# Attention and involution on one core: how the sums of exponentials get across the partitions in the first three images

## The chip, the cores and the metric

The kernel runs on one core of a Trainium2 chip. The metric is the device time in microseconds, the median of several runs of the same program; lower is better. The engines are TensorE (PE, with its weight loads shown apart as PEld), VectorE (DVE), ScalarE (ACT), GpSimd (POOL) and the DMA queues, most of them issued by SyncE (SP).

## What is computed

Input `x` has 4 images of 512 channels and 64 x 64 pixels in float32. Two layers follow each other. The reference, cut:

```python
# layer 0: attention over the 4096 pixels of an image, 128 inner channels
q, k, v = (einsum('oc,bcn->bon', w, xf) + b[:, None] for w, b in ...)
attn = softmax(einsum('bci,bcj->bij', q, k), axis=-1)
out = einsum('bcj,bij->bci', v, attn)
x = einsum('oc,bcn->bon', wo, out) + bo[:, None] + x
# layer 1: involution, 7 x 7 taps, groups of 16 channels
o1 = relu(affine(conv1x1(x, W1), s1, b1))
w  = conv1x1(relu(affine(conv1x1(o1, Wr), sr, br)), Ws) + bs
y  = sum over the 49 taps of w[group, tap, pixel] * o1[channel, pixel shifted by the tap]
out = affine(conv1x1(y, W3), s3, b3) + x
```

The softmax is computed without subtracting a maximum. (A check at the end of the kernel branches to a second, general path where the sums leave a safe interval; with these inputs that path is not taken.)

## The kernel before

**Attention.** The images are worked on one after the other. For each, `keys_values` makes the keys (`pk`) and values (`pv`) of all 4096 pixels. Then `attention` goes through eight chunks of 512 queries, numbered 0 to 7. A chunk has 32 steps. Step j makes one block of scores for 128 keys (`pss`, a matmul with 512 columns), ScalarE takes the exponential (`pt`, L797), and TensorE adds values times exponentials to `po`. The scores run two steps ahead. VectorE adds each `pt` to `pacc` (L826, L828, and for the last step to `sums`, L831), so that at the end of a chunk `sums` holds, for each of its 128 partitions, partial sums of the exponentials of 512 queries.

**The end of a chunk.** `finish_block` is a generator, started at the end of the chunk and advanced between the steps of the next one, one `yield` at a time; `chores()` does it once a step. It copies `po` to `on` (ScalarE, L651). It adds up `sums` over the partitions: L654, a VectorE reduction with a built-in transposition in blocks of 32 x 32, leaves in `blocks` 16 columns, and in each quarter of 32 partitions the sums over that quarter alone. In the kernel before, a matmul with `quads` (a matrix of ones wherever two partitions have the same place in their quarters) then adds the four quarters, and every partition gets the total (`pl`). After that come the reciprocal (L663, into `rls`), a transposition that spreads it over the columns (`spread` in PSUM, L666), and the product `on` times `spread` (L670). Next are the output projection (`pwo`) with the residual added on VectorE (L679), `p1` with its ReLU on ScalarE (L699), a transposition of the result into pixels and its way out by DMA (L732), and `pr`, which makes the units of the involution available.

The pauses in it differ between images. In the last image (`late`) they wait until a planned time; in the first three they are a number of `yield`s: three between the reduction and `pl`, five between the product `on` and the residual.

**Involution.** A unit is 4 lines of an image, 16 units an image. `involution` records its taps between the attention's steps: VectorE makes a product (L427, out of PSUM tile `pw` with the weights, of which there is one buffer), GpSimd adds it to `acc` (L447) and at the end folds it (L462). Then VectorE transposes the unit's sums (`turned`, L508), two DMAs finish the transposition, and `py` (TensorE) with its eviction on VectorE (L577) closes a chunk of output.

**What sets the order.** The program is recorded in the order of the generators, and a scheduler then places each engine's instructions by its own estimates; the engines work through their queues in order. How fast the taps are recorded is set by a planner: `pe` is the planned time of TensorE, `free["dve"]` and `free["pool"]` are the planned times when VectorE and GpSimd come free, `takes(engine, us)` adds work to them, and a tap waits while VectorE is planned to be 3.5 us or more behind.

**Buffers.** `pl`, `spread`, `pwo`, `p1`, `pr`, `py` and the queries (`pq`, made in step 23 or so of the chunk before) take turns in two PSUM banks (tag `mm`). `po` and `pacc` have one bank each. Five buffers hold exponentials.

Of the kernel before, what the change touches and what calls it, by code (L numbers as in the profile page):

```python
# [8 lines left out]
F32 = mybir.dt.float32  # L9
AF = mybir.ActivationFunctionType  # L10
ALU = mybir.AluOpType
# [4 lines left out]
P = 128  # L16
CT = C // P
CH = 512
# [62 lines left out]
TB = 32  # L81
# [8 lines left out]
def fast_path(  # L90
# [20 lines left out]
    nc = tc.nc  # L111

    def pool(name, bufs, **kw):
        return ctx.enter_context(tc.tile_pool(name=name, bufs=bufs, **kw))
# [6 lines left out]
    work2 = pool("work2", 2)  # L121
# [5 lines left out]
    ps = pool("ps", 2, space=bass.MemoryType.PSUM)  # L127
# [15 lines left out]
    quads = const.tile([P, P], F32, name="quads")  # L143
# [24 lines left out]
    free = {"dve": 0.0, "pool": 0.0, "dma": 0.0}  # L168
# [8 lines left out]
    def until(us):  # L177
        while pe < us and not tail:
            yield "wait"

    def pe_us(us):
        nonlocal pe
        pe += us
# [27 lines left out]
    def takes(engine, us):  # L211
        free[engine] = max(free[engine], pe) + us
        return free[engine]
# [39 lines left out]
    def mm(o, lhsT, rhs, start=True, stop=True, shared=1):  # L253
        pe_us(rhs.free_size() * PE_COLUMN / shared)
        return nc.tensor.matmul(o, lhsT=lhsT, rhs=rhs, start=start, stop=stop)  # L255
# [380 lines left out]
    def finish_block(b, c, off, n, po, sums):  # L636

        late = b == B - 1
        direct = late and c >= DIRECT
        name = f"{b}_{c}_{off}"  # L640
        xt = xs[b, c][:, :, off : off + n]

        def pause(us, steps):
            if late:
                yield from until(us + HOP_US)
            else:
                for _ in range(steps):
                    yield

        on = work2.tile([P, CH], F32, tag="on", name=f"on_{name}")[:, :n]  # L650
        nc.scalar.copy(on, po)  # L651
        blocks = work2.tile([P, CH // TB], F32, tag="blocks", name=f"blocks_{name}")
        takes("dve", DVE_OP)
        nc.vector.tensor_reduce(  # L654
            blocks, sums.rearrange("p (k q) -> p k q", q=TB), AX.X, ALU.add, apply_transpose=True
        )
        yield from pause(free["dve"], 3)
        pl = ps.tile([P, CH // TB], F32, tag="mm", name=f"pl_{name}")[:, : n // TB]
        for i in range(CH // n):
            mm(pl, quads, blocks[:, i * n // TB : (i + 1) * n // TB], i == 0, i == CH // n - 1)  # L660
        row = (b * N + c * CH + off) // TB
        rl = rls[:, row : row + n // TB]
        nc.vector.reciprocal(rl, pl)  # L663

        spread = ps.tile([P, CH], F32, tag="mm", name=f"spread_{name}")[:, :n]
        nc.vector.transpose(  # L666
            spread.rearrange("p (k q) -> p k q", q=TB),
            rl.unsqueeze(2).broadcast_to([P, n // TB, TB]),
# [59 lines left out]
        else:  # L728

            blocks = o1t.rearrange("p t c -> p (t c)")  # L730
# [48 lines left out]
    def attention(b, kt, vT, q):  # L779
# [22 lines left out]
        for m, (k, j) in enumerate(steps):  # L802
# [22 lines left out]
            if j == 0:  # L825
                nc.vector.tensor_copy(paccs[k], pt)  # L826
            elif j < nj - 1:
                nc.vector.tensor_tensor(paccs[k], paccs[k], pt, ALU.add)  # L828
            else:
                sums = work1.tile([P, CH], F32, tag="sums", name=f"sums_{b}_{k}")  # L830
                nc.vector.tensor_tensor(sums, paccs.pop(k), pt, ALU.add)  # L831
                f = finish_block(b, c, off, n, pos.pop(k), sums)
                next(f)
                finishing.append(f)
# [445 lines left out]
```

## Time and profile before

| | |
|---|---|
| median of 3 runs | 2587.23 us (2586.75 to 2587.34) |
| profiled execution | 2587.14 us, of which span 2585.2 us |
| granted TensorE clock | 0.999 |
| TensorE busy | 2570.4 us, 99% of the span |
| VectorE busy | 1862.6 us, 72% |
| GpSimd busy | 1825.2 us, 71% |
| ScalarE busy | 838.2 us, 32% |
| mean DMA rate | 94 GB/s |

The span runs from the first instruction to the last of the profiled execution; the time around it belongs to the launch. A matmul in float32 is carried out in two passes, and each shows as one weight load and one MATMUL row. The durations of matmuls are modelled, so their starts are what is read here. In the rows, `out<-in` names what is written and what is read; an idle time in brackets is followed by what ended it. "issue" is time in which an engine waited for nothing that the profile shows.

Chunk boundaries can be found by the copies of `po` (L651): in image 0 they begin at 125.87, 193.25, 260.63, 332.49, 405.84, 476.00, 547.86 and 616.30 us.

### The profile page before, as it was taken

The page shows a single profiled execution, that of the slowest core. Times are in us where ns is not written, and L with a number is a line of the kernel's source. Part 1 is how long each engine was busy: PE and PEld are TensorE (multiplying, and loading weights), DVE is VectorE, ACT ScalarE, POOL GpSimd, SP SyncE. Part 2 cuts the span into 40 slices and gives each one's busy share as a digit, 9 for nine tenths or more (in the row PEclk, how much of TensorE's full clock was granted, in tenths as well). Part 3 has the DMA queues.
Part 4 walks back from the last instruction along what each step waited for, and adds up shares of the span by engine and source line. Part 5 has one row for each costly group of instructions (what it writes and reads, how often), then busy time and mean ns, then how long its engine had stood idle before and what let it go on. Part 6 is the DMA issues. An engine that isn't in the chain of part 4 may idle for free.

```text
span 2585.2 us, 24342 instructions
## 1 busy us (share of the span) xinstructions
PE 2570.4 (99%) x7367; PEld 1229.3 (48%) x7367; DVE 1862.6 (72%) x2678; ACT 838.2 (32%) x1386; POOL 1825.2 (71%) x1207
## 2 busy tenths in 40 slices
PE   9999999999999999999999999999999999999998
PEld 7444444445544444444554444444465444444476
DVE  0347778887585777888667667878857678787888
ACT  1333333332233333333223333333322333333331
POOL 0006788877881778888786368888788567887887
PEclk9999999999999999999999999999999999999999
DMA  6033233445615343234661434433364431332343
GB/s 238 1 74 62 58 77 83 98 102 148 151 60 114 64 102 69 68 81 99 166 153 41 108 69 96 102 70 92 79 181 112 110 90 47 90 78 61 78 95 101
DMA packets 209049, 243.36 MB, mean 94 GB/s; under 512 B 109640, under 2 KB 129040, under 8 KB 208784
## 3 DMA queue, kind: packets, MB, share of 16 engines
q1 hardware_dynamic: 208480, 241.39, 38.9%
q8 instruction: 59, 0.97, 0.2%
q14 instruction: 78, 0.64, 0.1%
q10 hardware_dynamic: 432, 0.36, 0.1%
HBM read 192.65 MB, written 49.06 MB: 93 GB/s over the span
## 4 chain that ended last, share of the span: by engine, by line
PE 92%; POOL 4%; DVE 3%; issue 1%; ACT 0%; DVEq 0%; POOLq 0%
PE pss L255 32%; PE po L255 31%; PE pv L255 4%; PE pk L255 4%; PE pq L255 4%; PE p L255 4%; PE pwo L255 4%; PE py L255 4%; POOL acc L447 4%; PE pw L255 2%; DVE prod L427 1%; DVE pacc L828 1%; PE pr L255 1%; PE pa L259 1%; POOL acc L462 0%
## 5 line engine op out<-in xcount | busy, mean ns | idle before, releaser
L447 POOL TENSOR_TENSOR acc<-acc,prod 128x768 f32<-128x768 f32 (+3 forms) x1052 | 1682.8, 1617 | 737.9 <-DVE prod L427 694.6
L255 PE MATMUL pss<-q,k 128*128 128x512 f32 (+1 forms) x2112 | 1055.7, 584 | 0.0
L255 PE MATMUL po<-pt,v 128*128 128x512 f32 (+1 forms) x2112 | 1047.3, 580 | 0.0
L797 ACT ACTIVATE pt<-pss 128x512 f32<-128x512 f32 x1024 | 611.1, 597 | 1242.6 <-PE pss L255 1188.8
L427 DVE TENSOR_TENSOR prod<-ring,pw 128x768 f32<-128x768 f32 (+3 forms) x1086 | 874.7, 840 | 46.0 <-POOL acc L447 44.9
L828 DVE TENSOR_TENSOR pacc<-pacc,pt 128x512 f32<-128x512 f32 x958 | 664.8, 694 | 237.9 <-ACT pt L797 209.9
L255 PEld LDWEIGHTS po<-pt,v 128*128 128x128 f32 x2112 | 398.8, 190 | 480.9 <-issue 460.4
L255 PEld LDWEIGHTS pss<-q,k 128*128 128x128 f32 x2112 | 391.4, 190 | 466.8 <-issue 462.0
L508 DVE STREAM_TRANSPOSE turned<-acc 128x256 f32<-128x256 f32 x48 | 21.4, 445 | 217.9 <-POOL acc L462 217.9
L255 PE MATMUL py<-accT,wt 128*128 128x512 f32 (+1 forms) x256 | 130.1, 590 | 4.5 <-DVE x L577 4.5
L255 PE MATMUL pwo<-on,wt 128*128 128x512 f32 (+1 forms) x264 | 128.6, 580 | 0.1
L462 POOL TENSOR_TENSOR acc<-acc 128x512 f32<-128x512 f32 x122 | 121.4, 995 | 9.6
L255 PEld LDWEIGHTS pv<-wt,x 128*128 128x128 f32 x1024 | 119.6, 192 | 15.3 <-issue 15.1
L577 DVE SCALAR_TENSOR_TENSOR x<-py,vec,x 128x512 f32<-128x512 f32 (+2 forms) x136 | 96.4, 711 | 36.2 <-PE py L255 35.7
L255 PE MATMUL pv<-wt,x 128*128 128x128 f32 x1024 | 120.2, 275 | 0.0
L255 PE MATMUL p<-x,wt 128*128 128x512 f32 (+1 forms) x264 | 119.3, 580 | 0.0
L255 PE MATMUL pk<-x,wt 128*128 128x512 f32 x256 | 117.1, 596 | 0.0
L706 ACT ACTIVATE x<-x,vec 128x512 f32<-128x512 f32 (+1 forms) x132 | 92.9, 706 | 74.2 <-PE p L255 58.1
L255 PE MATMUL pq<-x,wt 128*128 128x512 f32 (+1 forms) x264 | 115.3, 579 | 0.0
L679 DVE SCALAR_TENSOR_TENSOR x<-pwo,bo,x 128x512 f32<-128x512 f32 (+1 forms) x132 | 95.1, 727 | 21.3 <-PE pwo L255 19.9
L427 DVE TENSOR_TENSOR acc<-ring,pw 128x1024 f32<-128x1024 f32 (+1 forms) x85 | 78.7, 945 | 15.6 <-PE pw L255 15.6
L255 PEld LDWEIGHTS pq<-x,wt 128*128 128x128 f32 x264 | 50.1, 190 | 59.7 <-issue 56.4
(74 smaller groups left out, 727.0 us busy)
## 6 DMA issues: line engine op xcount, KB each, us to landing
x<-x_dram SPq DMA_DIRECT2D x55, 1024.0 KB, 5.7
ring<-pix SPq DMA_DIRECT2D x74, 448.0 KB, 7.0
ring<-pix SPq DMA_DIRECT2D x24, 1344.0 KB, 9.7
out_dram<-x SPq DMA_DIRECT2D x31, 1024.0 KB, 4.5
ring<-pix SPq DMA_DIRECT2D x24, 896.0 KB, 10.5
ring<-pix SPq DMA_DIRECT2D x30, 672.0 KB, 10.9
ring<-pix SPq DMA_DIRECT2D x6, 2240.0 KB, 19.5
pix<-o1t SPq DMA_DIRECT2D x192, 32.0 KB, 1.7
```

Of the source, the lines that this page charges most:

```text
L255: return nc.tensor.matmul(o, lhsT=lhsT, rhs=rhs, start=start, stop=stop)
L259: nc.tensor.matmul(o, lhsT=lhsT, rhs=ident, start=start, stop=stop, is_transpose=True)
L427: product = (nc.gpsimd if maker == "pool" else nc.vector).tensor_tensor(made.rearrange("p t d (g c) -> p t d g c", g=G), image.rearrange(" ...
L447: nc.gpsimd.tensor_tensor(acc[:, these, d0 : d0 + n, :], acc[:, these, d0 : d0 + n, :], prod[:, :nt, :n, :], ALU.add,)
L462: nc.gpsimd.tensor_tensor(acc[:, :, :n, :], acc[:, :, :n, :], acc[:, :, n : 2 * n, :], ALU.add)
L508: nc.vector.transpose(blocks.rearrange("p (t k q) -> p t k q", t=NT, q=TB), acc[:, :, 0, :].rearrange("p t (k q) -> p t k q", q=TB),)
L577: nc.vector.scalar_tensor_tensor(xt[:, t, :], py, v1(V_S3 + t), xt[:, t, :], ALU.mult, ALU.add)
L679: nc.vector.scalar_tensor_tensor(xt[:, t, :], pw, bo[:, t : t + 1], xt[:, t, :], ALU.add, ALU.add)
L706: nc.scalar.activation(xt[:, t, :], xt[:, t, :], AF.Identity, bias=v1(V_B3 + t))
L797: nc.scalar.activation(pt, pss, AF.Exp)
L828: nc.vector.tensor_tensor(paccs[k], paccs[k], pt, ALU.add)
```

## The change

In images 0 to 2 the four quarters are no longer added by the matmul. VectorE copies `blocks` into the first columns of the PSUM tile `spread`, adds each quarter's neighbour to it (four adds on 32 partitions of 16 columns), copies the pair sums to PSUM again, adds the other pair's (two adds on 64 partitions), and takes the reciprocal in place in `rls`. The second operand of an add lies in PSUM, so that it can come from other partitions. The three pauses ahead of `pl` are gone in these images, and the whole chain up to the product `on` is recorded in one go at the end of the chunk. The planner is told of 1 us more on VectorE. In the last image nothing changes.

```diff
         blocks = work2.tile([P, CH // TB], F32, tag="blocks", name=f"blocks_{name}")
+        blocks2 = work2.tile([P, CH // TB], F32, tag="blocks2", name=f"pairs_{name}")
         takes("dve", DVE_OP)
         nc.vector.tensor_reduce(
             blocks, sums.rearrange("p (k q) -> p k q", q=TB), AX.X, ALU.add, apply_transpose=True
         )
-        yield from pause(free["dve"], 3)
-        pl = ps.tile([P, CH // TB], F32, tag="mm", name=f"pl_{name}")[:, : n // TB]
-        for i in range(CH // n):
-            mm(pl, quads, blocks[:, i * n // TB : (i + 1) * n // TB], i == 0, i == CH // n - 1)
+        if late:
+            yield from pause(free["dve"], 3)
         row = (b * N + c * CH + off) // TB
         rl = rls[:, row : row + n // TB]
-        nc.vector.reciprocal(rl, pl)
+        if late:
+            pl = ps.tile([P, CH // TB], F32, tag="mm", name=f"pl_{name}")[:, : n // TB]
+            for i in range(CH // n):
+                mm(pl, quads, blocks[:, i * n // TB : (i + 1) * n // TB], i == 0, i == CH // n - 1)
+            nc.vector.reciprocal(rl, pl)
 
         spread = ps.tile([P, CH], F32, tag="mm", name=f"spread_{name}")[:, :n]
+        if not late:
+            cols = n // TB
+            other, pairs = spread[:, :cols], blocks2[:, :cols]
+            nc.vector.tensor_copy(other, blocks)
+            for i in range(P // TB):
+                mine, next_ = (slice(j * TB, (j + 1) * TB) for j in (i, i ^ 1))
+                nc.vector.tensor_tensor(pairs[mine], blocks[mine], other[next_], ALU.add)
+            nc.vector.tensor_copy(other, pairs)
+            for i in range(2):
+                mine, next_ = (slice(j * 2 * TB, (j + 1) * 2 * TB) for j in (i, i ^ 1))
+                nc.vector.tensor_tensor(rl[mine], pairs[mine], other[next_], ALU.add)
+            nc.vector.reciprocal(rl, rl)
+            takes("dve", 1.0)
         nc.vector.transpose(
             spread.rearrange("p (k q) -> p k q", q=TB),
             rl.unsqueeze(2).broadcast_to([P, n // TB, TB]),
```

## Prediction

> **What bounds the kernel now.** I read the page first: busy time, then the chain that ended last.
>
> ```profile
> PE 2570.4 (99%) x7367; PEld 1229.3 (48%) x7367; DVE 1862.6 (72%) x2678; ACT 838.2 (32%) x1386; POOL 1825.2 (71%) x1207
> ...
> PE 92%; POOL 4%; DVE 3%; issue 1%; ACT 0%; DVEq 0%; POOLq 0%
> ```
>
> TensorE carries 92% of the chain, and POOL and DVE carry only the tail. Cut into stages, the profile has TensorE busy for 1827.02 of the 1831.00 us between 129 and 1960 us, which are images 0 to 2 after the first keys. So there a matmul less is time gained, and every wait that is put before a matmul is time lost. The order of the changed kernel's instructions is the same as before from chunk 1 of image 3 on, on TensorE, so the tail stays; all that follows is three times the same image.
>
> Then TensorE's timeline around one `pl`:
>
> ```profile
> 128.33 1.02 PE L255 MATMUL po<-pt,v 128*128 128x512 f32 x2
> 129.19 0.29 PE L255 MATMUL pl<-blocks,quads 128*128 128x16 f32 x2
> 129.33 1.10 PE L255 MATMUL pss<-q,k 128*128 128x512 f32 x2
> 130.27 0.59 PE L255 MATMUL po<-pt,v 128*128 128x512 f32 x1
> ```
>
> A product of 512 columns starts every 0.86 us (128.33 to 129.19; I use 0.859). From one `po` to the next lie 1.94 us here where a pair without `pl` takes 1.72: `pl` costs 0.22 us, more than its 0.14 alone, since its second weight load cannot hide behind so short a product.
>
> Third, what TensorE's waits are. The four idle microseconds of that stage are three of these, one in each image:
>
> ```profile
> 379.24 0.65 PE L255 MATMUL pr<-o,wt 128*64 128x256 f32 x4
> 381.02 1.12 PE L255 MATMUL py<-accT,wt 128*128 128x512 f32 x2 [1.12 <-DVE x L577]
> 382.36 0.93 PE L255 MATMUL pw<-wt,red 33*128 33x392 f32 x4 [0.22 <-DVE prod L427]
> ```
>
> The second `py` of chunk 4 wants the PSUM buffer of the first, whose eviction (L577) is late in VectorE's queue.
>
> Last, VectorE at the end of a chunk, the tightest one:
>
> ```profile
> 406.04 0.68 DVE L831 TENSOR_TENSOR sums<-pacc,pt 128x512 f32<-128x512 f32 x1
> 406.75 0.71 DVE L654 TRANSPOSE_TENSOR_REDUCE blocks<-sums 128x16 f32<-128x512 f32 x1
> 407.39 0.67 DVE L826 COPY pacc<-pt 128x512 f32<-128x512 f32 x1
> ...
> 411.03 0.25 DVE L663 RECIPROCAL rls<-pl 128x16 f32<-128x16 f32 x1
> ...
> 412.00 0.71 DVE L666 STREAM_TRANSPOSE spread<-rls 128x512 f32<-128x512 f32 x1
> ...
> 413.48 0.67 DVE L670 TENSOR_TENSOR on<-on,spread 128x512 f32<-128x512 f32 x1
> ```
>
> `on` is ready at 414.15; the weights of the first `pwo` load at 417.54, 3.4 us later. Over the 24 chunks this margin is 3.4 to 6.8 us, and it is what the change spends.
>
> **Removed: 24 `pl`.** 24 x 0.22 = 5.3 us, all on the path. Nothing hides it.
>
> **Moved: the residual, three steps earlier.** Without the three pauses the first `pwo` stands after step 3 or 4 of the next chunk (4 in chunks 3, 4, 6; 3 in 0, 1, 2; one product earlier than 4 in 5), where it stood after step 6. `p1`, `pr`, the pixel DMAs and the units follow; the DMAs have 11 steps or more to their reader in both orders, so I cost them at nothing. Counted from the copy of `po` (405.84 in the chunk shown), the slot of the first `pwo` was 417.54 - 405.84 = 11.70 us. It becomes 11.70 - 0.22 - 4 x 0.859 = 8.04 for chunks 3, 4, 6, 6.3 for 0 to 2, 7.2 for 5.
>
> **Moved with it: the late eviction of `py`.** In the new order `pr` and the first `py` stand together at step 18, the second `py` at step 20 behind other buffers, and the first eviction has four steps. The wait of 1.12 us and what surrounds it go. Its price is read from the copies of `po`: chunks 2 to 3 and 5 to 6 are 71.86 us apart (332.49 - 260.63, 547.86 - 476.00), chunks 3 to 4 are 73.35 (405.84 - 332.49). 1.49 x 3 = 4.5 us. What may be late next: the queries of step 23 need the buffer of the second `py`, whose eviction stands behind the transposition that waits for POOL's last fold (L508; 204.6 us of waits on VectorE in this stage). In the chunk above that transposition began 19.6 us before the copy, and about 19.4 is needed. The units start about 2 us earlier in the new order, which gives that margin.
>
> **Added: eight small VectorE instructions a chunk,** in one chain from the reduction to `on`. The trace has none of them. The nearest rows: an add of 128x4 took 0.164 us, the reciprocal of 128x16 took 0.25; the adds of 512 columns take 0.694 but start every 0.605, so 0.09 overlap. Lower end 0.09 each (all overlapped), 0.7 us a chunk; upper end 0.28 each (the reciprocal and a dependent start, 0.03), 2.2 us. Less than nothing is excluded: no instruction goes from VectorE. I take 0.19, from the add, the nearest row: 1.5 us. 24 x 1.5 = 36 us more on VectorE, 72% to 73.5%: no bound.
>
> The Trainium skill ("VectorE: DVE Perf Modes", on two Vector instructions with no wait between them) speaks against this: an instruction whose operands start in another group of 32 partitions than those of the one before waits until all earlier ones have finished. By it the six adds would not overlap, nor would the next large instruction, some 0.2 us a chunk more than my value; the sum for the path would change only in chunks without margin. No row here shows such adds.
>
> **Does `on` come in time?** In the new order of chunks 3, 4 and 6, five adds of the next chunk and one tap product stand among the chain. From the start of `sums`: 0.71 + 0.64 + 0.57 for sums, reduction, copy; 5 x 0.605 adds; 0.86 product (407.96 to 408.82); 0.16 reciprocal (to its successor); 0.63 transposition; 0.67 product; 1.5 small ones: 8.8 us (8.0 to 9.5). Chunk 5: 7.7 to a slot of 7.2. Chunk 2: 7.3 to 6.3. Chunks 0, 1 and 7 have no taps in the way and microseconds of margin.
>
> So it hangs on when `sums` starts, relative to the copy of `po`: -3.6 us in chunks where VectorE only waits for exponentials, +0.2 in the chunk shown, the latest of all. VectorE is backlogged from the transposition (386.25) to `sums` (406.04). In the new order its queue there holds 1.5 to 5 us more work, but the unit before began earlier (step 8 for 10 or 11), so the transposition is earlier too. By these I get starts at about -3 (chunk 3), -1.5 (4), -2 (5), -1 (6), and in chunk 2 -3: `on` at 5.8, 7.3, 5.7, 7.8, 4.3 against 8.0, 8.0, 7.2, 8.0, 6.3. It just fits; chunk 6 has 0.2 us. I allow 0.7 us of waits an image, 2 us.
>
> **Sum.** Profiled execution 2587.14 (span 2585.2, 1.9 around it; the median of three is 2587.23, 0.1 more): 2587.2 - 5.3 - 4.5 + 2 = 2579.4. Below all this lies 2577.4 with no wait at all.
>
> **Rivals.** *The matmul alone.* The wait of `py` does not go but moves to the queries, or small waits of 1.5 us an image before `pwo` eat it: 2587.2 - 5.3 = 2581.9, and up to 2592 as these waits grow to 5 us an image. For it: L508's waits of up to 7.3 us. Against: the units' earlier start.
>
> *`on` is late: slower.* One mechanism: the chain ends after the slot of the first `pwo`, and TensorE stands; behind the waiting `pwo` queue the next scores, and ScalarE's exponentials and VectorE's adds wait for those. If `sums` starts at +0.2 in chunks 2 to 6, as in the tightest chunk now, and a small instruction takes 0.28: 0.2 + 9.5 - 8.0 = 1.7 in chunks 3, 4, 6; 0.2 + 8.4 - 7.2 = 1.4 in 5; 0.2 + 8.0 - 6.3 = 1.9 in 2. That is 8.4 an image, 25 us, and 2602 in all. It decides from 3.3 us an image (9.8 / 3) on. For it: 3.4 us of margin in the tightest chunk are less than the 3.66 by which its slot moves. Against: `on` no longer waits for `pl` (VectorE waited 9.8 us for it in this stage) and the earlier units.
>
> *VectorE or POOL becomes the bound:* it would need some 500 us more; no chance worth a number.
>
> **Chances.** A measurement of this kernel can tell some 0.2%, 5.2 us, from no change. The forecast (both gains, under 1.5 us of waits an image) 0.6; the matmul alone or less 0.26, of which 0.02 beyond 0.2%; late `on` beyond its gain 0.14. Faster by over 0.2% (below 2582.1): 0.62; within: 0.24; slower: 0.14. The range goes from 2576.5, just under the case without waits, to 2590, which takes in most of the second case and leaves out the third.
>
> **What would show it.** Right: no `pl` before 1960 us, TensorE's 1.12 us waits for L577 gone, chunks 71.6 us apart, small adds of 0.16 to 0.2 us. Wrong: weight loads of `pwo` that wait for L670's successor, weight loads of `pq` that wait for L577's, each with its lateness; then chunks 2 to 6 are longer than 0 and 1.

## The result, and the profile after

| | before | after |
|---|---|---|
| median | 2587.28 us (6 runs) | 2605.78 us (2604.09 to 2608.14, 6 runs) |
| ratio after to before | | 1.0071, 95% interval 1.0058 to 1.0083 |
| profiled execution | 2587.14 us, span 2585.2 | 2608.14 us, span 2606.3 |
| first and last (24th) copy of `po` of images 0 to 2 | 125.87, 1881.22 us | 126.58, 1900.76 us |

The changed kernel is slower by 0.7%; the forecast was 2579.4 us. The medians are 18.5 us apart. The profiled executions, of which that of the changed kernel is the slowest of its six, are 21.1 us apart in span, of which 18.8 lie between the first and the 24th copy of `po` (1774.18 us for 1755.35). The start is 0.7 us later, image 3 is 0.4 shorter, and 1.9 come behind the last work of any compute engine.

The page, its busy times and its chain that ended last:

```profile
PE 2575.7 (99%) x7319; PEld 1228.4 (47%) x7319; DVE 1898.9 (73%) x2870; ACT 838.1 (32%) x1386; POOL 1823.6 (70%) x1207
...
PE 76%; POOL 9%; DVE 8%; issue 5%; DMA 1%; SPq 0%; ACT 0%; POOLq 0%; DVEq 0%
```

The 48 rows that `pl` took from TensorE are gone (7319 for 7367), VectorE has 192 more, and its busy time rose by 36.3 us. That it is close to the 36 of the prediction is in part luck: the eight new instructions of a chunk make 32.2 us of it, and the tap products, which overlap less than before, another 7.0 (881.7 us for 874.7), while smaller groups fell. But the chain has moved: TensorE carries 76% of it instead of 92%, and VectorE and GpSimd 17% instead of 7%. TensorE now waits for them, and the waits between 129 and 1985 us say where (engine, what it was to do, whom it waited for: us in all, times, longest):

```profile
DVE prod L427 <- POOL acc L447: 72.7, 109, 2.0
...
PEld pwo L255 <- DVE on L686: 30.7, 16, 4.3
...
PE pwo L255 <- DVE on L686: 17.8, 14, 3.5
```

The same two kinds of wait before the change, in the same stretch:

```profile
DVE prod L427 <- POOL acc L447: 32.0, 53, 1.8
...
PE py L255 <- DVE x L577: 3.3, 3, 1.1
```

The wait of `py` for L577 is gone. In its place the first `pwo` of a chunk waits for the product `on` (L686): `on` is late. Above it stands a wait that is more than twice what it was: VectorE's tap products wait for one of the four buffers that GpSimd must empty.

Both are seen in chunk 5, the worst one. VectorE's timeline from its tap products to `on`:

```profile
466.48 4.40 DVE L427 TENSOR_TENSOR prod<-ring,pw 128x1024 f32<-128x1024 f32 x5
470.80 0.69 DVE L844 TENSOR_TENSOR pacc<-pacc,pt 128x512 f32<-128x512 f32 x1
472.67 0.69 DVE L427 TENSOR_TENSOR prod<-ring,pw 128x512 f32<-128x512 f32 x1 [1.18 <-POOL acc L447]
473.27 0.69 DVE L844 TENSOR_TENSOR pacc<-pacc,pt 128x512 f32<-128x512 f32 x1
475.10 0.42 DVE L427 TENSOR_TENSOR prod<-ring,pw 128x256 f32<-128x256 f32 x1 [1.13 <-POOL acc L447]
476.45 0.69 DVE L427 TENSOR_TENSOR prod<-ring,pw 128x512 f32<-128x512 f32 x1 [0.93 <-POOL acc L447]
...
480.89 0.68 DVE L847 TENSOR_TENSOR sums<-pacc,pt 128x512 f32<-128x512 f32 x1
481.61 0.71 DVE L655 TRANSPOSE_TENSOR_REDUCE blocks<-sums 128x16 f32<-128x512 f32 x1
482.24 0.67 DVE L842 COPY pacc<-pt 128x512 f32<-128x512 f32 x1
482.82 0.15 DVE L672 COPY spread<-blocks 128x16 f32<-128x16 f32 x1
483.01 0.70 DVE L844 TENSOR_TENSOR pacc<-pacc,pt 128x512 f32<-128x512 f32 x1
483.75 0.71 DVE L675 TENSOR_TENSOR pairs<-blocks,spread 32x16 f32<-32x16 f32 x4
...
488.36 0.69 DVE L686 TENSOR_TENSOR on<-on,spread 128x512 f32<-128x512 f32 x1
```

GpSimd in the same stretch works without a pause, so its pace is what VectorE waits for:

```profile
467.83 16.25 POOL L447 TENSOR_TENSOR acc<-acc,prod 128x1024 f32<-128x1024 f32 x12 [1.71 <-DVE prod L427]
```

The copy of `po` was at 477.83. So `sums` starts 3.1 us after it, where the prediction had it 2 us before it. And TensorE, at the same place:

```profile
484.58 1.02 PE L255 MATMUL pss<-q,k 128*128 128x512 f32 x2
489.10 2.08 PE L255 MATMUL pwo<-on,wt 128*128 128x512 f32 x2 [3.51 <-DVE on L686]
490.97 1.92 PE L255 MATMUL po<-pt,v 128*128 128x512 f32 x2
492.68 1.91 PE L255 MATMUL pss<-q,k 128*128 128x512 f32 x2
494.38 1.35 PE L255 MATMUL po<-pt,v 128*128 128x512 f32 x2
495.57 1.02 PE L255 MATMUL pwo<-on,wt 128*128 128x512 f32 x2
```

After 3.5 us of idling, the next seven passes take twice their time: the pairs start 1.87, 1.71 and 1.70 us apart instead of 0.86. The granted clock is 0.5 for 6.83, 3.41 and 3.41 us in the three images; it falls 0.9 us before this `pwo` in image 0, and 1.1 and 0.6 us after it in images 1 and 2. Before the change there was no half clock between 129 us and the last three microseconds.

Added up over images 0 to 2: `pwo` starts late by 20.3 us in all (TensorE's start-to-start distances ahead of it, less a normal pass), the half clock costs 6.3, `pl` gives 5.3 and the wait of `py` 4.4. That makes 16.9 of the 18.8 us; 1.9 us are spread over small distances and not assigned.

### The profile page after: what moved, and what is told of

Its sections match the earlier page's. It is cut to its first block, busy times and chain, and to the rows that moved or that the text cites. A ratio compares the mean times of both kernels' runs of the same rounds, so it can differ in the third digit from the quotient of the medians.

```text
span 2606.3 us, 24446 instructions
## 1 busy us (share of the span) xinstructions
PE 2575.7 (99%) x7319; PEld 1228.4 (47%) x7319; DVE 1898.9 (73%) x2870; ACT 838.1 (32%) x1386; POOL 1823.6 (70%) x1207
## 4 chain that ended last, share of the span: by engine, by line
PE 76%; POOL 9%; DVE 8%; issue 5%; DMA 1%; SPq 0%; ACT 0%; POOLq 0%; DVEq 0%
PE pss L255 26%; PE po L255 26%; POOL acc L447 8%; PE pwo L255 4%; PE p L255 4%; PE pk L255 3%; PE py L255 3%; PE pq L255 3%; DVE pacc L844 3%; PE pv L255 3%; DVE prod L427 3%; PE pw L255 2%; POOL acc L462 1%; PE pa L259 1%; PE pr L255 1%
## 5 line engine op out<-in xcount | busy, mean ns | idle before, releaser
L447 POOL TENSOR_TENSOR acc<-acc,prod 128x768 f32<-128x768 f32 (+3 forms) x1052 | 1681.3, 1616 | 758.7 <-DVE prod L427 717.2
L427 DVE TENSOR_TENSOR prod<-ring,pw 128x768 f32<-128x768 f32 (+3 forms) x1086 | 881.7, 842 | 89.9 <-POOL acc L447 84.4
L508 DVE STREAM_TRANSPOSE turned<-acc 128x256 f32<-128x256 f32 x48 | 21.4, 445 | 172.7 <-POOL acc L462 172.7
L577 DVE SCALAR_TENSOR_TENSOR x<-py,vec,x 128x512 f32<-128x512 f32 (+2 forms) x136 | 96.1, 709 | 30.4 <-PE py L255 29.1
L255 PEld LDWEIGHTS pwo<-on,wt 128*128 128x128 f32 x264 | 48.5, 191 | 79.7 <-issue 44.4
## 6 DMA issues: line engine op xcount, KB each, us to landing
ring<-pix SPq DMA_DIRECT2D x30, 672.0 KB, 10.8
```

Source lines behind the costliest of these rows:

```text
L427: product = (nc.gpsimd if maker == "pool" else nc.vector).tensor_tensor(made.rearrange("p t d (g c) -> p t d g c", g=G), image.rearrange(" ...
L447: nc.gpsimd.tensor_tensor(acc[:, these, d0 : d0 + n, :], acc[:, these, d0 : d0 + n, :], prod[:, :nt, :n, :], ALU.add,)
L508: nc.vector.transpose(blocks.rearrange("p (t k q) -> p t k q", t=NT, q=TB), acc[:, :, 0, :].rearrange("p t (k q) -> p t k q", q=TB),)
L577: nc.vector.scalar_tensor_tensor(xt[:, t, :], py, v1(V_S3 + t), xt[:, t, :], ALU.mult, ALU.add)
```

## Experiments

Theory: `on` is late because `sums` is late, and `sums` is late because VectorE waits for GpSimd's buffers while the slot of `pwo` came three steps forward. Rivals: the eight small instructions themselves, the missing pauses ahead of them, or one chunk alone.

### Parts undone: the pauses, the place of the residual, one chunk

`e1_pauses_back`, against the changed kernel:

```diff
-        if late:
-            yield from pause(free["dve"], 3)
+        yield from pause(free["dve"], 3)
```

> The adds stay on VectorE; the three pauses between the reduction and the adds come back, so that the first pwo stands after step 6 of the next chunk again. Theory 1 (the slot): the loss is TensorE's wait at a first pwo that was moved three steps ahead of an `on` that could not follow (20 us in the trace), and the half clock behind the longest of these waits (6 us). Then both go, and what is left is the gain of the removed matmuls: 2587.3 - 5.3 = 2582, with up to 3 us either way for the new order of py. No wait of pwo for `on` in the trace. Theory 2 (the instructions): eight small instructions a chunk, which hold up their neighbours, make VectorE late for all that hangs on it, wherever the residual stands. Then it stays at 2600 or more.

Measured: 2592.25 us, ratio 1.0015 (1.0006 to 1.0025), between the two theories. The waits of `pwo` went, as the residual then stands three steps later again; in their place came waits of `py` for L577, 7.6 us in two, with the half clock behind each.

`e2_residual_back`, which keeps the chain early and puts only the residual back:

```diff
-            yield from pause(spreads, 5)
+            yield from pause(spreads, 8)
```

> As the changed kernel, with the adds recorded at the end of the chunk without pauses, but eight pauses in place of five between the product `on` and the residual: the chain starts as early as it can, and the first pwo stands after step 6 as in the kernel before. Theory 1: `on` is ready 9 to 11 us after the copy of po, the slot is at 11.5: no waits, 2582, within 3 us, and no half clock. Theory 2: 2600 or more.

Measured: 2617.13 us, 1.0110 (1.0093 to 1.0127). A miss: the time is what theory 2 had, but the waits of `pwo` are gone. In their place `py` waits for L577, 20.9 us in five: this order puts the eviction of its buffer far back in VectorE's queue, at the end of an image and of the next image's first chunk. TensorE's timeline at one of them:

```profile
754.33 1.02 PE L255 MATMUL po<-pt,v 128*128 128x512 f32 x2
761.77 2.08 PE L255 MATMUL py<-accT,wt 128*128 128x512 f32 x2 [6.41 <-DVE x L577]
763.63 1.53 PE L255 MATMUL pss<-q,k 128*128 128x512 f32 x2
```

`e3_chunk5_back`, the residual at its old place in chunk 5 only:

```diff
-            yield from pause(spreads, 5)
+            yield from pause(spreads, 8 if c == 5 else 5)
```

> As the changed kernel, with eight pauses in place of five for chunk 5 alone. Chunk 5 has the longest wait (3.7 us in each image), and the half clock follows it alone. Theory 1: 3 x 3.7 us of waits and about 3 x 2 us of half clock go, some 17 us: 2588 to 2590, with the short waits of chunks 2, 3, 4 and 6 (0.3 to 1.05 us) still there and the clock at full rate throughout images 0 to 2. If a short wait also brought the half clock, it would still show. Theory 2: 1 us an image at most, 2603.

Measured: 2594.96 us, 1.0025 (1.0013 to 1.0037): 10.8 us less than the changed kernel, 5 us above the range of theory 1. The profiled execution (2592.71 us) has no half clock before the tail. Of TensorE's waits at `pwo` 6.9 us in 10 are left, the longest 0.9. So one chunk in eight made over half of the loss, and the rest is spread over the others.

### The early slot without the small adds

`e4_matmul_early_residual` is the kernel before, with the matmul and its pauses, and the residual three steps earlier:

```diff
-            yield from pause(spreads, 5)
+            yield from pause(spreads, 2)
```

> The kernel before, with the matmul and its three pauses, but two pauses in place of five between `on` and the residual: the first pwo stands after step 3, as in the changed kernel, and no small add is there. Theory 1: `on` was ready 5.4 to 8.4 us after the copy of po, the slot is now at 6.5, so waits of 0 to 2 us or more a chunk come with the matmul too: 2592 to 2615. Theory 2: without the adds no loss, 2585 to 2588.

Measured: 2659.51 us, 1.0278 (1.0261 to 1.0295). The waits between 129 and 1985 us:

```profile
PEld pwo L255 <- DVE on L670: 56.4, 12, 11.2
DVE prod L427 <- POOL acc L447: 54.3, 84, 2.0
...
PE pwo L255 <- DVE on L670: 47.0, 11, 10.4
```

With no small add in it the early residual loses 71 us against the kernel before, about four times as much as the changed kernel and more than either theory had. So such a loss needs no small adds: the early place, with all that it moves, is enough. What the adds themselves do in the changed kernel this run does not say.

### What the planner is told

The line `takes("dve", 1.0)` does nothing on the chip. It tells the planner of 1 us more work, and the planner spreads the taps by it. Three kernels are without it: `e8_changed_untold` is the changed kernel less that line; `e5_adds_alone` has the edit of `e1` too, so that TensorE's order is that of before but for `pl`; `e6_chain_early` has the edit of `e2` too, the chain early and the residual at its old place.

```diff
-            takes("dve", 1.0)
```

> The changed kernel without the 1 us that the planner was told of; the first pwo stays at its early place. Theory 1: taps are recorded about 1 us earlier, ahead of sums and the chain, so the waits of pwo for `on` stay or grow: 2600 to 2615. If the planner's extra microsecond is what spoils the order, it falls to about 2585.

> The adds on VectorE with the three pauses ahead of them back, and without the 1 us that the planner was told: TensorE's instructions then stand in the same order as in the kernel before, with only pl missing, and the adds stand where pl stood. Theory 1, widened by the runs before (what costs is where VectorE's queue stands behind GpSimd when TensorE needs it, and the order decides that): the order is the old one, so the old waits alone remain (one py an image, 1.1 us), no half clock before the tail, and 24 x 0.22 us are gained: 5.3 us below the kernel before. Theory 2 (the adds themselves cost): slower than the kernel before by some microseconds, with waits at pwo or py that the kernel before did not have.

> As the run with the residual put back behind eight pauses, without the 1 us that the planner was told. The chain stands at the end of the chunk in one go, TensorE's order is that of the kernel before within four instructions. If the 29 us of that run came from the chain's place, this one is slow too, over 2600; if they came from the order that the planner made of the extra 1 us (py evictions behind GpSimd at the end of an image), they go: 5 us below the kernel before, within 3 us.

Measured: `e8` 2638.66 us, 1.0200 (1.0184 to 1.0215), with `pwo` waiting up to 6.5 us; `e5` 2592.24 us, 1.0018 (1.0009 to 1.0027); `e6` 2584.79 us, 0.9988 (0.9978 to 0.9997).

Without the line the changed kernel loses 33 us more, above the expected range. With the residual back, the same line is worth 32 us the other way (`e2` with it 2617.13, `e6` without it 2584.79). One microsecond in the plan decides where taps and `py` fall, and that is worth more than the matmul. `e6` is the first kernel that beats the one before, and by little: its wait of `py` grew from 1.1 to 1.5 us, and that is enough for the half clock to come at times. TensorE's waits of 2.1 us for `py` in `e5` show it better: of its eleven runs two have a mean granted clock of 0.999 and 2584.3 and 2586.7 us (the profiled one is of these), the other nine have 0.996 and 2592 to 2594 us. By its letter `e5` meets its second theory. TensorE's and GpSimd's orders are those of the kernel before, `pl` apart, so the longer wait comes from the adds: between the copies of chunks 3 and 4 of image 0, counted from the first of them, the eviction that `py` waits for starts 0.8 us later (48.5 for 47.7), and the `py` itself would stand 0.2 us earlier.

### The buffers between VectorE and GpSimd

`e7_six_products` is the changed kernel with six buffers for the tap products; `e9`, `e10` and `e11` are `e6`, the kernel before and `e5` with six; `e12` is `e7` with the residual one step later.

```diff
-    prods = pool("prods", 4)
+    prods = pool("prods", 6)
...
-            yield from pause(spreads, 5)
+            yield from pause(spreads, 6)   # e12 alone
```

> The changed kernel with six buffers for tap products in place of four; the order of the instructions is the same within a few. In chunk 5 the products waited for GpSimd to free a buffer (5 times, 4 us in all) ahead of sums. If that is why sums came 3 us after the copy of po, two more buffers take these waits away, sums comes at about 0, the wait of pwo in chunk 5 falls from 3.7 to under 1 us, and the half clock goes: 15 us less, about 2590. If sums is late for another reason (the exponentials, the work in VectorE's queue), it stays at 2604 to 2608.

> The chain at the end of the chunk with the residual at its old step (the run that beat the kernel before by 2.4 us), and six buffers for tap products in place of four. What held its py (1.5 us in each image, and half clock after it) were taps ahead of the eviction that waited for GpSimd to free a buffer. Theory 1: with six buffers the eviction is on time, the py wait and the half clock go, and both gains stand alone: 2587.2 - 5.3 - 4.4 = 2577.5, no half clock before the tail. If the adds cost VectorE something that TensorE feels beyond these waits, it stays above 2582.

> The kernel before, matmul and all, with six buffers for tap products. It says what the buffers are worth without the change. Theory 1: the three py waits of 1.1 us and what surrounds them go, 4.4 us: 2582.8. If the buffers are worth nothing by themselves: 2587.

> The adds in the place of the matmul, in the old order of TensorE, with six buffers for tap products. Its twin with four was 5 us slower than the kernel before in most executions, with py waits of 2.1 us and half clock. Theory 1: the adds cost only through these waits; `on` was ready 0.6 us or more before pwo, so with six buffers 2577.5, as the run with the early chain. Theory 2 (the adds themselves): it stays above 2582.8, the kernel before with six buffers.

> The changed kernel with six buffers for tap products and six pauses in place of five ahead of the residual: the first pwo stands one step, 1.72 us, later than in the run with six buffers alone, where `on` was late by up to 1.8 us. Theory 1: these waits shrink to about 0.1 us, 2578 to 2582, unless the new order puts another instruction that TensorE needs behind GpSimd.

Measured: `e7` 2593.40 us (1.0024, 1.0014 to 1.0034), `e9` 2587.40 (0.9997, 0.9988 to 1.0006), `e10` 2591.88 (1.0016, 1.0007 to 1.0025), `e11` 2589.72 (1.0007, 0.9998 to 1.0016), `e12` 2593.73 (1.0024, 1.0014 to 1.0033). The changed kernel gained 12.4 us, 3 us short of its expectation; `e9` to `e12` missed theirs by 9 to 12 us. The waits of `e7`, in the stretch and form of above:

```profile
PEld pwo L255 <- DVE on L686: 13.7, 17, 2.4
DVE prod L427 <- POOL acc L447: 13.0, 21, 0.9
...
PE pwo L255 <- DVE on L686: 5.9, 5, 1.6
```

`sums` of chunk 5 starts 1.2 us after the copy of `po` instead of 3.1. But the others did not gain, or lost. The time from the last copy of `po` to the end tells why: 53.6 us in the kernel before, 62.3, 61.4, 59.9, 59.6 and 59.3 in these five. From the first to the 24th copy each of the five is 1.7 to 5.8 us shorter than the kernel before (`e12` loses 3.3 us again in image 3). So six buffers help while attention runs and hurt in the tail, where the scheduler puts the instructions in another order: 100 of TensorE's 303 rows behind the last copy of `po` stand elsewhere. TensorE's longest wait there, for a product that GpSimd makes, is 2.7 us in each of the five and 0.3 in the kernel before, and there are one or two stretches of half clock (3.41 us each; two in `e9`), which the kernel before has only in its last 3 us. The tail also puts `e9` above 2582 us, where its second theory (the adds themselves) had it. For `e11` that theory is not excluded: with the old tail it would end at some 2583.3 us (2528.0 to the last copy, 53.5 behind it, 1.8 of launch), against the 2582.8 that the theory named, and its queries wait 3.7 us for an eviction. The last three runs test this: six buffers up to the end of attention, and the old four in the tail.

```diff
     prods = pool("prods", 4)
+    more = pool("more", 2)
+    sixth = iter(range(1 << 30))
...
                     home = tailpools[1] if maker == "dve" else prods
+                    if not tail and next(sixth) % 6 > 3:
+                        home = more
```

`e13` is so made from the changed kernel, `e14` from `e6`, `e15` from the kernel before. TensorE, VectorE and GpSimd have the same instructions in the same order as in these twins, so the buffers are all that differs.

> The changed kernel, with six buffers for the tap products up to the end of the attention and the old four in the tail (two more in a pool of their own, taken in turn). Theory: VectorE's wait for GpSimd's buffers is what makes `sums` late in images 0 to 2, and the loss that six buffers brought lies only in the last 55 us (62.3 us from the last copy of `po` to the end with six, against 53.6 with four), where products and adds are dealt out otherwise. Then the last copy of `po` comes at 2529.3 us as with six, the end 53.5 us later, and the time is about 2584.7 us. Rival: the last 55 us are longer because image 3 begins in another state (GpSimd further behind or ahead), whatever the buffers of the tail: 2592 to 2594 us as with six throughout.

> The small adds and the chain early, residual at its old place, planner not told, six buffers up to the tail and four in it. Theory: last copy of `po` at 2526.3 us as with six, the end 53.5 us later, 2581.7 us in all: faster than before by 5 to 6 us, and than the same with four buffers by 3. Rival (the state at the start of image 3): 2587 us as with six throughout.

> The kernel before (matmul, pauses, residual late) with six buffers up to the tail and four in it. Theory: 2529.9 + 53.5 + 1.9 = 2585.3 us, 2 us faster than before, as the waits of `py` shrink only in part. Rival (the state at the start of image 3): 2592 us as with six throughout.

Measured: `e13` 2586.66 us, 0.9995 (0.9986 to 1.0004); `e14` **2581.01 us, 0.9973 (0.9963 to 0.9983)**; `e15` 2585.60 us, 0.9990 (0.9981 to 0.9999). The theory's three numbers (2584.7, 2581.7, 2585.3) are met within 2 us, the rival's (2592 and more, 2587, 2592) are not. `e14` and `e15` end 53.3 and 53.7 us after the last copy of `po`; `e13` takes 55.7, and its compute engines' work there is that of before to 0.1 us, so those 2 us lie behind the last of it.

The waits of `e13`, then of `e14`, in the stretch and form of above:

```profile
DVE prod L431 <- POOL acc L451: 13.0, 21, 0.9
...
PE pwo L257 <- DVE on L690: 6.7, 6, 1.6
```

```profile
DVE prod L431 <- POOL acc L451: 9.8, 15, 0.9
...
PE pq L257 <- DVE x L581: 2.9, 3, 1.0
```

No `pwo` waits for `on` in `e14`, and what is left of the late eviction is a wait of the queries:

```profile
384.59 1.02 PE L257 MATMUL py<-accT,wt 128*128 128x512 f32 x2
386.59 3.70 PE L257 MATMUL pq<-x,wt 128*128 128x512 f32 x8 [0.97 <-DVE x L581]
```

`e14` against `e15` is the gain of the small adds in place of the matmul, with the chain early, where little is late: 4.6 us. Between the first and the 24th copy of `po` it is 3.9 us, near the 5.3 of the 24 `pl` less 0.4 in each image, by which the wait of the queries is longer (1.0 us for 0.6). `e13` against `e15` is the change as it was made, with six buffers: 1.1 us slower, still no gain.

## Why the prediction was wrong

**Right: the matmul.** A `pl` was worth 0.22 us. Chunks 0 to 1 of image 0, where nothing waits, are 67.15 us apart instead of 67.38, and 24 times that is about the 5.3 us forecast; `e14` against `e15` shows 4.6 of it in the end. The slot of the first `pwo` was right too: its weights load 6.32 us after the copy where nothing waits, for 6.3. TensorE's order becomes that of before in chunk 2 of image 3 and not in chunk 1, which cost nothing: image 3 is 0.4 us shorter.

**Right: the wait of `py`.** The 1.12 us waits for L577 are gone in the changed kernel, and no query waits for it. That it can move to the queries, as the first rival had it, is shown by `e14`.

**Right, a little short: the small instructions.** The groups of the small instructions in the changed kernel, forms apart (busy us, mean ns of one, idle time before):

```profile
L675 DVE TENSOR_TENSOR pairs<-blocks,spread 32x16 f32<-32x16 f32 x96 | 16.1, 167 | 1.8
L679 DVE TENSOR_TENSOR rls<-pairs,spread 64x16 f32<-64x16 f32 x48 | 8.1, 169 | 1.1
L680 DVE RECIPROCAL rls<-rls 128x16 f32<-128x16 f32 x24 | 6.1, 253 | 0.8
L676 DVE COPY spread<-pairs 128x16 f32<-128x16 f32 x24 | 4.1, 170 | 0.3
L672 DVE COPY spread<-blocks 128x16 f32<-128x16 f32 x24 | 3.9, 161 | 0.3
```

The adds and copies take 0.16 to 0.17 us, where 0.19 was taken for each with what surrounds it. Four adds on the four quarters take 0.71 us, and the next large add starts 0.74 after the first of them (483.75 to 484.49 in the timeline above): they do not overlap, nor does their neighbour. That is what the Trainium skill says ("VectorE: DVE Perf Modes", on two Vector instructions with no wait between them) of operands that start in another group of 32 partitions. From the start of `sums` to the end of `on` it made 9.1 us in chunks 3, 4 and 6 for the 8.8 of the prediction, 8.2 in 5 for 7.7, 7.5 in 2 for 7.3: 0.2 to 0.5 us a chunk.

**Wrong: when `sums` starts.** This is the step that failed. Its start against the copy of `po`, and VectorE's waits for GpSimd's buffers between the transposition (L508) and `sums`, in us (image 0):

| chunk | 2 | 3 | 4 | 5 | 6 |
|---|---|---|---|---|---|
| taken by the prediction | -3 | -3 | -1.5 | -2 | -1 |
| changed kernel | -1.8 | +0.04 | +0.3 | +3.1 | +0.05 |
| of it, waits for buffers | 0 | 1.1 | 1.1 | 3.8 | 1.1 |
| `e13`, six buffers | -1.1 | -1.2 | -1.05 | +1.1 | -1.2 |
| `e13`, waits for buffers | 0 | 0 | 0 | 2.1 | 0 |

So `pwo` was late by 6.2, 6.9 and 7.2 us in the three images, where 0.7 us an image was allowed. The prediction reasoned that the unit before starts earlier, so that the transposition is earlier too, and gave VectorE's queue 1.5 to 5 us more work behind it. Both held in chunks 3 to 6: the transposition starts 21.3 to 22.4 us before the copy instead of 17.9 to 20.9, and VectorE has 1.5 to 4.9 us more work from there to `sums`. Left out was a resource. VectorE took 21.7 to 25.4 us for 19.8 to 20.3 us of its own work, most of the difference in waits of its tap products for one of GpSimd's four buffers. The two costliest groups of the pair, on the page of the changed kernel (busy us, mean ns of one, idle time before and who ended most of it):

```profile
L447 POOL TENSOR_TENSOR acc<-acc,prod 128x768 f32<-128x768 f32 (+3 forms) x1052 | 1681.3, 1616 | 758.7 <-DVE prod L427 717.2
...
L427 DVE TENSOR_TENSOR prod<-ring,pw 128x768 f32<-128x768 f32 (+3 forms) x1086 | 881.7, 842 | 89.9 <-POOL acc L447 84.4
```

A product takes 0.84 us in the mean and its add on GpSimd 1.62, so a burst of products can run ahead of GpSimd only by as many as there are buffers. That VectorE's 32.0 us of waits for L447 stood in the trace before was a warning: they were not in the sum. `e7` and `e13` show it by giving two buffers more: the waits fell from 72.7 to 13.0 us, `sums` of chunk 5 from +3.1 to +1.2 (`e7`) and +1.1 us (`e13`), and the time with `e13` by 19.1 us (2605.78 to 2586.66), to that of the kernel before.

The buffers are not all of the miss. Their waits cover 1.1 of its 3.0 us in chunk 3, 1.1 of 1.8 in chunk 4, 3.8 of 5.1 in chunk 5 and all of it in chunk 6; in chunks 3 to 5 the rest lies in how the queue was added up, which the prediction gives only as results, and in up to 1.4 us of waits for exponentials and `py`; no run separates these. In chunk 2 no buffer is waited for. There a tap product waits 0.9, 1.6 and 2.2 us in the three images for the DMA that brings its pixels (`ring`), a wait of at most 0.2 us in the kernel before; the prediction had put these DMAs at nothing. And "microseconds of margin" in chunks 0, 1 and 7 held in chunk 1 and in chunk 0 of image 0 alone: in chunk 7, and in chunk 0 of images 1 and 2, the weights of `pwo` load 0.05 us after `on` ends, and that chunk 0 loses 0.7 us each time.

`e13` still has 6.7 us of TensorE's waits at `pwo`: the slot three steps earlier is too early for 9 us of chain even so, and `e14`, with the old slot, has none.

**Wrong: what a wait costs.** The prediction priced a wait at its length. The three of 3.5 us cost another 6.3 us through the clock. The rival "`on` is late" had the mechanism, and 2602 us for `sums` at +0.2 and slow small instructions in all five chunks. `sums` did start at +0.04 to +0.3 in chunks 3, 4 and 6, but `pwo` was late by 0.75 to 1.05 us there and not by 1.7; that the time came near is in part luck, made by one chunk at +3.1 and the clock.

## What to carry to other kernels

A step's earliest time is set by every queue behind it, not by the one that issues it: where a producer feeds a slower consumer through a few buffers, an earlier start can be lost in waits for them, and the waits for these buffers that stand in the profile belong into the sum. Take the slack of a step chunk by chunk from the trace and give it away only where more is left than the neighbour's backlog can move; an instruction saved on the busiest engine can be worth less than the place of those behind it (here 5.3 us against 20.3). Where a change moves work past others, keep the old place and make the saving alone first, and see what else that delays: with four buffers it lost 5.0 us (`e5`), and with six in the attention and the chain early it gained 4.6 (`e14` against `e15`).

## What the runs showed of the hardware

**After a long enough idle time TensorE runs at half its clock.** Over the seventeen traces, TensorE's idle times between 129 and 1985 us of at least 0.6 us sort like this: of 41 up to 1.2 us none was followed by passes at half speed; of 15 between 1.2 and 1.7, two; of three between 1.7 and 2.5, one; of 20 longer ones, all. The half clock lasted 3.41 us or a multiple. The Trainium skill ("TensorE: Matmul & The Clock Gate", the part on the clock gate) states half rate after at least one idle window of about 3.4 us, in windows that run freely. The lengths of the slow stretches agree with that; the idle time needed does not, and these runs decide here: 2.64 to 2.81 us were enough in `e2` each time, and 1.5 us at times in `e6`. So a wait on TensorE of 2.6 us or more costs more than its length: by the slow passes (0.85 instead of 0.43 us each), 2.9, 1.7 and 1.7 us more in the changed kernel's three.

**More buffers can cost, through the order.** Six buffers instead of four in the tail made the last 55 us 6 to 8 us longer (`e14` against `e9`, `e15` against `e10`: 53.3 for 61.4, 53.7 for 59.9). The order of the instructions changed with the buffers, TensorE waited 2.7 us for a product of GpSimd, and half clock followed; how much each of these costs was not separated.
